# A third Strassen level for one of seven small products, with its sums on GpSimd

## Chip, cores and metric

The kernel runs on one core of a Trainium2 chip. The metric is device time in microseconds. Three runs of the kernel before took 819.62, 819.81 and 820.03 us; their median is 819.81 us.

## The reference

Everything is float32. For four sequences of 1024 tokens with 1024 features the kernel computes a layer norm, then two branches, a gated linear recurrence `s` and a two-expert routed feed-forward `ffn`, and returns `x + s * silu(ffn)`.

```python
xn = layernorm(x)
# recurrence branch
g   = sigmoid(xn @ gate_w.T + gate_b)
u_g = xn * g
aa  = tanh(a);  G = cumprod(aa over time)
s   = c * (G * cumsum(b * u_g / G_safe, time)) + (d + mean_t(u_g) @ d_lr_u @ d_lr_v / R) * u_g
# feed-forward branch
gates, idx = top2(softmax(xn @ wr.T)), normalised
h = silu(xn @ w1.T);  h = silu(h @ w3.T);  h = h @ w2.T
out = zeros;  for k in 0, 1:  out = out.at[idx[:, k]].add(gates[:, k] * h)
return x + s * silu(ffn)
```

The expert index addresses rows of the output, so only rows 0 to 7 of `out` receive anything. All other rows of the result are `x`. Those eight rows depend on all 4096 tokens through w1 and w3, and on the gate product of the first 1024.

## The kernel before

The tokens are taken in four groups of 1024 (`sb` 0 to 3, `NS = 4`). In each group there are two large products of 1024 x 1024 x 1024: `u` (times w1) and `m` (times w3). Group 0 also has `g` (times the gate weights). Each large product is done by Strassen's method in Winograd's form, twice nested.

**The outer level** makes seven products of 512 x 512 x 512 of each large one. The code calls each of them a Half. It has a kind, a group and an index i from 1 to 7, taken in the order `(1, 2, 5, 6, 7, 4, 3)` for u and `(1, 5, 6, 2, 7, 4, 3)` for m. Their left operands are blocks of tokens or the sums of blocks `s1` to `s4`; the right operands are blocks of weights or sums kept from group 0. A block is 128 partitions x 4 quarters x 512 elements.

**The inner level** makes seven small products of 256 x 256 x 256 of each Half, in the steps n = 0 to 6 of `Half.step`. Each is four matmuls of 128 x 128 x 256, issued by `small`. Left inner sums (`left_sums`, four per Half, on GpSimd) and right inner sums (computed in group 0, stored, and read back as quarters by `load_kept_sum`) are tiles of one quarter.

The small products go to PSUM banks. X takes steps 0, 2, 4 and 6 of a Half, Z steps 1 and 5, Y step 3. X and Z have two banks each, Y one. After each step VectorE (or, where a destination is new, ScalarE) reads the bank and adds it to the destination block (`first`, `more`). `whole` then runs the outer sums of the results, and SiLU on ScalarE when a quarter of the result is complete.

**The order** is written out by hand. Every engine's instructions keep the order in which the program emits them. A Half starts 7 places after the one before it, and its step n stands at its start + 2n, so two Halves interleave: the order of small products round a junction is step 6 of Half h-1 (place start + 5 of Half h), step 3 of Half h (start + 6), step 0 of Half h+1 (start + 7), step 4 of Half h (start + 8), step 1 of Half h+1 (start + 9). One place is one small product. The X bank of step 0 of Half h+1 is the one that step 6 of Half h-1 has used, and can be written once that step's result has been read. Work of the other engines is put between by `at(place, f)`: `left_sums` at start - 6, -4, 0 and +2, the loads of kept sums 9 places ahead of their use, and the outer sums of tokens `s1` to `s4` at places tied to the Halves that need them.

`s_engine` (line 779) says which engine makes the outer sums of the left side: GpSimd for u in groups 1 to 3, VectorE for the rest. In m of groups 1 to 3 these are 16 sums of 128 x 512 per group on VectorE.

Tiles of a block or a quarter come from two lists in rotation (`NB, NQ = 20, 18`, line 125). A released tile goes to the end of the list, and whoever takes it next waits for its last reader. All loads and stores of weights and tokens are issued on SP's queue, in order.

Of the kernel before, what the change touches and what calls it, by code (L numbers as in the profile page):

```python
# [10 lines left out]
F32 = mybir.dt.float32  # L11
# [3 lines left out]
ALU = mybir.AluOpType  # L15
AX = mybir.AxisListType
P = 128
Q = 256
# [4 lines left out]
def kernel(  # L23
# [55 lines left out]
    class Pinned:  # L79
# [15 lines left out]
    nc = tc.nc  # L95
    pe, dve, act, pool, sync = (
        Pinned(e) for e in (nc.tensor, nc.vector, nc.scalar, nc.gpsimd, nc.sync)
    )
# [7 lines left out]
    ps_y = ctx.enter_context(tc.tile_pool(name="ps_y", bufs=1, space=bass.MemoryType.PSUM))  # L106
# [15 lines left out]
            if self.uses == 0:  # L122
                self.home.append(self.tile)

    NB, NQ = 20, 18
    IDLE = 13
    blocks = deque(
        const.tile([P, 4, 2 * Q], F32, tag=f"b{i}", name=f"b{i}") for i in range(NB)
# [8 lines left out]
    def quarter(uses=1):  # L137
        return Held(quarters, uses)
# [47 lines left out]
    def at(place, f, *args):  # L186

        seq[0] += 1
        heapq.heappush(todo, (place, seq[0], f, args))
# [8 lines left out]
    def resume(p, g):  # L198
        step = next(g, None)
        if step is not None:  # L200
            at(p + step, resume, p + step, g)
# [14 lines left out]
    start = {}  # L216
# [301 lines left out]
    kept = {}  # L518
    op_t = {}
# [14 lines left out]
    def keep_quarter(name, i, j, o):  # L534
        d = dramp.tile([P, 2 * Q], F32, tag=f"{name}_{i}_{j}", name=f"{name}_{i}_{j}")
        sync.dma_start(d, o.tile)
        kept[name, i, j] = d
        o.drop()
# [177 lines left out]
    def first_w3():  # L716
# [48 lines left out]
    S_OF = {  # L765
        1: (0, 0),
        2: (0, 1),
        4: (1, 1),
        5: "s1",
        6: "s2",  # L770
        3: "s4",
        7: "s3",
    }
    left = {}
# [2 lines left out]
    A_AT = (1, 2, 4, 5)  # L777

    def s_engine(kind, sb):
        return pool if kind == "u" and sb > 0 else dve  # L780


    BANKS = {("u", 0): (0, 1), ("m", 0): (0,)}
# [1 line left out]
    def s1(kind, sb, n):  # L785
        eng = s_engine(kind, sb)
        a21, a22 = left[kind, sb, (1, 0)], left[kind, sb, (1, 1)]
        o = block(1 + n)
        if (kind, sb) in BANKS:
            yield from with_bank(o, a21, a22, (3, 0, 1, 2), op=ALU.add, of=BANKS[kind, sb])  # L790
        else:
            for q in (3, 0, 1, 2):
                eng.tensor_tensor(o[:, q], a21[:, q], a22[:, q], ALU.add)
                if q == 0:
                    yield 0.5
        a21.drop()
        a22.drop()
        left[kind, sb, "s1"] = o

    def s2(kind, sb, n):  # L800
        eng = s_engine(kind, sb)
        while (kind, sb, "s1") not in left:
            yield 0.25
        p, a11 = left[kind, sb, "s1"], left[kind, sb, (0, 0)]
        o = block(2 * n)
        if (kind, sb) in BANKS:
            yield from with_bank(o, p, a11, (2, 3, 0, 1), of=BANKS[kind, sb])
        else:
            for q in (2, 3, 0, 1):
                eng.tensor_tensor(o[:, q], p[:, q], a11[:, q], ALU.subtract)  # L810
                if q == 3:
                    yield 0.5
        p.drop()
        a11.drop()
        left[kind, sb, "s2"] = o

    def s4(kind, sb, n):

        eng = s_engine(kind, sb)
        while (kind, sb, "s2") not in left:  # L820
            yield 0.25
        o, a12 = left[kind, sb, "s2"], left[kind, sb, (0, 1)]
        if (kind, sb) == ("m", 0):
            yield from with_bank(o, o, a12, (2, 3, 0, 1), True, of=(0, 2))
        else:
            for q in (2, 3, 0, 1):
                eng.tensor_tensor(o[:, q], a12[:, q], o[:, q], ALU.subtract)
                yield 0.5
        a12.drop()
        left[kind, sb, "s4"] = o  # L830
# [35 lines left out]
                yield 2 * (A_AT[j + 1] - A_AT[j])  # L866


    def small(ps, A, B, start, stop, rows_first):

        for mt in range(2):
            for kt in range(2):
                w, m = (A, B) if rows_first else (B, A)
                pe.matmul(
                    ps[:, mt * Q : (mt + 1) * Q],
                    w[:, kt * Q + mt * P : kt * Q + (mt + 1) * P],
                    m[:, kt * Q : (kt + 1) * Q],
                    start=(start and mt == 0 and kt == 0),
                    stop=(stop and mt == 1 and kt == 1),
                    skip_group_check=True,  # L880
                )
# [3 lines left out]
    class Half:  # L885
# [30 lines left out]
        def whole(self, q):  # L916
            whole(self.kind, self.sb, self.i, q)

        def step(self, n):
            if n == 0:  # L920
                self.begin()
            A, t = self.A, self.t
            ts = [op_ts.get((self.kind, self.sb, self.i, j)) for j in range(4)]
            s = [left_q.get((self.src, self.sb, self.i, j)) for j in range(4)]

            def go(ps, a, b, start, stop):
                small(ps, a, b, start, stop, self.rows_first)

            if self.plain:

                q = ((0, 1, 2, 3) if self.i == 1 else (0, 3, 1, 2))[n // 2]
                ps = self.X if n // 2 % 2 == 0 else self.Z
                go(ps, A[:, q // 2 * 2 + n % 2], t[:, n % 2 * 2 + q % 2], n % 2 == 0, n % 2 == 1)
                if n % 2:
                    self.first(q, ps)
            elif n == 0:
                go(self.X, A[:, 0], t[:, 0], True, False)
                self.first(0, self.X)
            elif n == 1:
                go(self.Z, s[0].tile, ts[0].tile, True, False)  # L940
                self.first(3, self.Z)
                s[0].drop()
                ts[0].drop()
            elif n == 2:
                go(self.X, s[1].tile, ts[1].tile, False, False)
                self.first(1, self.X)
                s[1].drop()
                ts[1].drop()
            elif n == 3:
                Y = ps_y.tile([P, 2 * Q], F32, tag="Y", name=f"Y_{self.tag}")  # L950
                go(Y, A[:, 1], t[:, 2], True, True)
                if (self.kind, self.i) == ("g", 1):
                    at(Y_AT, self.more, 0, Y)
                else:
                    self.more(0, Y)
            elif n == 4:
                go(self.X, s[2].tile, ts[2].tile, False, False)
                self.more(3, self.X)
                s[2].drop()
                ts[2].drop()  # L960
            elif n == 5:
                go(self.Z, s[3].tile, t[:, 3], False, True)
                self.more(1, self.Z)
                s[3].drop()
            elif n == 6:
                go(self.X, A[:, 3], ts[3].tile, False, True)
                self.first(2, self.X)
                self.whole(2)
                ts[3].drop()
            if n == (7 if self.plain else 6):  # L970
                self.A.drop()
                t.drop()
# [265 lines left out]
    for kind, sb, i, plain in line:  # L1238
        h = Half(kind, sb, i, plain)
        halves.append(h)  # L1240
        S = start[kind, sb, i]
        n = 2 if sb == 0 and kind == "u" and i not in PLAIN_G else 1
        if kind != "g" and not plain:
            at(S + 2 - 8, left_sums, kind, sb, i, n)
        if kind != "g" and sb > 0:
            at(S - 10, load_kept, kind, sb, i)
            for j in range(4):
                at(S + 2 * T_AT[j] - 9, load_kept_sum, kind, sb, i, j)

    for sb in range(NS):  # L1250
        n = 2 if sb == 0 else 1
# [252 lines left out]
```

## Time and profile before

| | us |
|---|---|
| median of three runs | 819.81 |
| span of the profiled execution | 817.9 |
| start of u and of m in group 1 | 266.4 and 358.4 |
| start of u and of m in group 2 | 443.2 and 535.2 |
| start of u and of m in group 3 | 620.0 and 712.1 |
| one Half of u or m | 12.1 |

For the profiled execution the span alone is given; what lies around it is the difference to the times of the runs, 1.9 us.

The six stages of groups 1 to 3, from the profile's windows (columns: stretch, its length, busy microseconds and instructions of TensorE, weight loads, VectorE, ScalarE and GpSimd, granted TensorE clock, share of the DMA engines, GB/s):

```
266.00:358.00 92.00, 92.00 (x492) 78.00 (x490) 45.34 (x90) 39.76 (x74) 53.43 (x43) 1.00 0.67 243
358.00:443.00 85.00, 85.00 (x396) 74.67 (x395) 64.31 (x82) 17.01 (x29) 44.01 (x33) 1.00 0.76 285
443.00:535.00 92.00, 92.00 (x491) 78.04 (x490) 41.01 (x87) 39.27 (x72) 51.11 (x41) 1.00 0.62 228
535.00:620.00 85.00, 85.00 (x396) 74.64 (x396) 64.12 (x82) 16.82 (x29) 44.18 (x33) 1.00 0.77 286
620.00:712.00 92.00, 92.00 (x491) 78.03 (x490) 41.43 (x88) 17.92 (x30) 50.88 (x41) 1.00 0.56 194
712.00:797.00 85.00, 85.00 (x416) 73.02 (x415) 52.73 (x85) 14.24 (x24) 34.48 (x27) 1.00 0.46 167
```

A row of a group of instructions reads: line, engine, operation, what is written from what (buffer numbers left out), partitions x elements, count; then busy time and the mean duration of one in ns; then the engine's idle time just before them and what ended it. All lines of code show as line 89, that of the helper which records every operation, so tiles tell groups apart: q is a quarter, b a block, X, Y and Z with `_u`, `_m`, `_g` the banks of a kind. A matmul in float32 shows as two records on TensorE (PE) with two weight loads (PEld). A record lasts until its results have landed, so the next one starts before it ends.

### The profile page before, as it was taken

How to read it: one execution, taken by the hardware profiler on the slowest of the kernel's cores; microseconds unless marked ns; L12 is line 12 of the kernel's file. 1: busy time of each engine (PE TensorE's matmuls, PEld its weight loads, DVE VectorE, ACT ScalarE, POOL GpSimd, SP SyncE). 2: the span in 40 equal slices, each digit the busy share in tenths (PEclk: the TensorE clock that was granted, in tenths of full speed). 3: DMA queues.
4: the chain of work that ended last, by engine and by line, in shares of the span. 5: the costliest groups of instructions: out<-in, count | busy, mean ns of one | idle time of the engine just before them, and what ended most of it. 6: DMA issues, size and time to landing. Idle time of an engine off the chain costs nothing.

```text
span 817.9 us, 11299 instructions
## 1 busy us (share of the span) xinstructions
PE 810.6 (99%) x4085; PEld 696.5 (85%) x4085; DVE 509.7 (62%) x868; ACT 263.8 (32%) x458; POOL 496.1 (61%) x398
## 2 busy tenths in 40 slices
PE   8999999999999999999999999999999999999997
PEld 7888888888888878888888788888888788888885
DVE  6886598765588524764985235666983246667643
ACT  1245126877232237341022065421122021220111
POOL 2799896967999394744547453755448454465300
PEclk9999999999999999999999999999999999999999
DMA  9946619465978947629955875559666365555700
GB/s 338 421 175 232 230 47 357 171 246 160 411 267 309 345 174 293 241 103 385 376 179 210 332 279 190 187 206 426 242 244 257 104 219 203 196 180 195 283 14 2
DMA packets 55927, 192.88 MB, mean 236 GB/s; under 512 B 6480, under 2 KB 9792, under 8 KB 44224
## 3 DMA queue, kind: packets, MB, share of 16 engines
q1 hardware_dynamic: 55552, 191.61, 63.5%
q8 instruction: 33, 0.54, 0.3%
q10 hardware_dynamic: 320, 0.54, 0.2%
q14 instruction: 22, 0.18, 0.1%
HBM read 169.01 MB, written 39.87 MB: 255 GB/s over the span
## 4 chain that ended last, share of the span: by engine, by line
PE 98%; DMA 1%; DVE 0%; ACT 0%; issue 0%; SPq 0%
PE X_u L89 24%; PE X_m L89 24%; PE Z_u L89 12%; PE Z_m L89 12%; PE X_g L89 6%; PE Y_m L89 6%; PE Y_u L89 6%; PE Z_g L89 3%; PE acc L89 2%; PE plT L89 2%; PE Y_g L89 1%; DMA b<-in_x 1%; PE pp L89 0%; DVE bn L89 0%; PE accB L89 0%; PE ta L89 0%
## 5 line engine op out<-in xcount | busy, mean ns | idle before, releaser
L89 POOL TENSOR_TENSOR q<-b 128x512 f32<-128x512 f32 x154 | 203.0, 1331 | 193.7 <-PE X_m L89 48.0
L89 ACT ACTIVATE b<-b 128x512 f32<-128x512 f32 (+1 forms) x152 | 105.3, 696 | 298.1 <-DVE b L89 291.6
L89 POOL TENSOR_TENSOR q<-b,q 128x512 f32<-128x512 f32 x98 | 133.1, 1361 | 7.2 <-issue 4.0
L89 POOL TENSOR_TENSOR b<-b,b 128x512 f32<-128x512 f32 x72 | 92.9, 1310 | 48.5 <-PE X_u L89 33.7
L89 DVE TENSOR_TENSOR b<-b,b 128x512 f32<-128x512 f32 x120 | 109.2, 925 | 2.7
L89 PE MATMUL X_m<-q,q 128*128 128x256 f32 x448 | 105.9, 379 | 0.0
L89 PE MATMUL X_u<-q,q 128*128 128x256 f32 x432 | 102.4, 380 | 0.0
L89 DVE TENSOR_TENSOR b<-X_u,b 128x512 f32<-128x512 f32 x87 | 60.0, 690 | 57.8 <-PE X_u L89 57.1
L89 DVE TENSOR_TENSOR b<-X_m,b 128x512 f32<-128x512 f32 x88 | 60.4, 688 | 56.9 <-PE X_m L89 56.7
L89 PEld LDWEIGHTS X_m<-q,q 128*128 128x128 f32 x448 | 85.0, 190 | 12.4 <-issue 0.8
L89 POOL TENSOR_TENSOR q<-q,b 128x512 f32<-128x512 f32 x56 | 73.6, 1314 | 32.4 <-PE X_u L89 25.1
L89 PEld LDWEIGHTS X_u<-q,q 128*128 128x128 f32 x432 | 81.8, 190 | 12.2 <-issue 1.2
L89 DVE TENSOR_TENSOR b<-b,bc 128x1024 f32<-128x1024 f32 x56 | 67.8, 1211 | 0.1
L89 PE MATMUL X_u<-b,b 128*128 128x256 f32 x248 | 58.4, 380 | 0.0
L89 PE MATMUL Y_m<-b,b 128*128 128x256 f32 x224 | 53.1, 380 | 0.0
L89 PE MATMUL Z_m<-b,q 128*128 128x256 f32 x224 | 53.0, 380 | 0.0
L89 PE MATMUL X_m<-b,b 128*128 128x256 f32 x224 | 53.0, 379 | 0.0
L89 PE MATMUL Z_m<-q,q 128*128 128x256 f32 x224 | 52.9, 379 | 0.0
L89 PE MATMUL X_m<-q,b 128*128 128x256 f32 x224 | 52.9, 379 | 0.0
L89 PEld LDWEIGHTS X_u<-b,b 128*128 128x128 f32 x248 | 47.0, 190 | 6.7 <-DVE b L89 0.4
L89 DVE TENSOR_TENSOR b<-Z_u,b 128x512 f32<-128x512 f32 x47 | 32.4, 690 | 31.6 <-PE Z_u L89 30.7
L89 PE MATMUL Z_u<-q,q 128*128 128x256 f32 x216 | 51.1, 380 | 0.0
(182 smaller groups left out, 1171.6 us busy)
## 6 DMA issues: line engine op xcount, KB each, us to landing
q<-w SPq DMA_DIRECT2D x168, 256.0 KB, 4.5
b<-in_w SPq DMA_DIRECT2D x36, 1024.0 KB, 9.0
b<-w_T SPq DMA_DIRECT2D x24, 1024.0 KB, 6.3
b<-in_xT SPq DMA_DIRECT2D x15, 1024.0 KB, 12.9
w<-q SPq DMA_DIRECT2D x56, 256.0 KB, 7.4
b<-in_x SPq DMA_DIRECT2D x12, 1024.0 KB, 11.0
w_T<-b SPq DMA_DIRECT2D x8, 1024.0 KB, 4.4
b<-in_gw SPq DMA_DIRECT2D x6, 1024.0 KB, 14.0
```

What stands on the lines that cost most here:

```text
L89: r = f(*args, **kwargs)
```

## The change

In groups 1 to 3, for u and m, step 3 (the product `A[:, 1]` times `t[:, 2]`) is split once more by the same method: seven products of 128 x 128 x 128 in place of four matmuls of 128 x 128 x 256.

- `token_thirds` makes the left sums of the third level, three instructions on GpSimd (one of 128 x 256, two of 128 x 128), at start - 2. `weight_thirds` makes the right sums, four of 128 x 128 on GpSimd at start - 3, in group 1 alone, and stores them. `load_thirds` reads them back in groups 2 and 3 on SP's queue.
- `Half.eighth` issues the products: two at start + 2, ahead of step 1; one at start + 4, ahead of step 2; and four in place of step 3 at start + 6. All go to the Y bank, which the Half now holds from start + 2. VectorE adds parts of the bank to the destination: two reads of 128 x 128 after the first visit, one after the second, one of 128 x 512 and one of 128 x 128 after the third, in place of the one of 128 x 512.
- `s_engine` puts the outer sums of m in groups 1 to 3 on GpSimd too.
- There are 24 quarters in rotation for 18, and the scratch area for dynamic DMA is set to 1024 bytes.

Over the whole program that is 126 matmuls more, 168 VectorE reads of the bank more and 48 outer sums fewer, and 230 GpSimd sums more (48 outer ones, 182 of the third level); 42 transfers of 256 KB are added.

```diff
-    NB, NQ = 20, 18
+    NB, NQ = 20, 24
...
     def s_engine(kind, sb):
-        return pool if kind == "u" and sb > 0 else dve
+        return pool if sb > 0 else dve
...
+    def is_third(kind, sb, i):
+        return sb > 0 and kind != "g"
+
+    def cut(t):
+        return t.rearrange("p (k n) -> p k n", n=P)
+
+    def token_thirds(kind, sb, i):
+
+        a = cut(left[kind, sb, S_OF[i]][:, 1])
+        t = quarter()
+        o = cut(t.tile)
+        third_s[kind, sb, i] = t
+        pool.tensor_tensor(
+            o[:, 0:2], a[:, 1:2].to_broadcast([P, 2, P]), a[:, 0::3], ALU.subtract
+        )
+        yield 1
+        pool.tensor_tensor(o[:, 2], a[:, 0], o[:, 1], ALU.subtract)
+        pool.tensor_tensor(o[:, 3], a[:, 2], o[:, 2], ALU.subtract)
+
+    def weight_thirds(kind, sb, i):
+
+        name = {"u": "w1", "m": "w3"}[kind]
+        b = cut(op_t[kind, sb, i][:, 2])
+        t = quarter(2)
+        o = cut(t.tile)
+        third_t[kind, sb, i] = t
+        pool.tensor_tensor(o[:, 1], b[:, 1], b[:, 0], ALU.subtract)
+        yield 1
+        pool.tensor_tensor(o[:, 2], b[:, 3], o[:, 1], ALU.add)
+        pool.tensor_tensor(o[:, 3], b[:, 2], o[:, 2], ALU.subtract)
+        yield 1
+        pool.tensor_tensor(o[:, 0], b[:, 1], b[:, 3], ALU.add)
+        yield 1
+        keep_quarter(name, i, "t", t)
+
+    def load_thirds(kind, sb, i):
+        o = quarter()
+        sync.dma_start(o.tile, kept[{"u": "w1", "m": "w3"}[kind], i, "t"])
+        third_t[kind, sb, i] = o
...
+        def eighth(self, n):
+            key = self.kind, self.sb, self.i
+            a, b = cut(self.A[:, 1]), cut(self.t[:, 2])
+            S, T = cut(third_s[key].tile), cut(third_t[key].tile)
+            d = cut(self.dst[:, 0])
+            z, w = (1, 2) if self.rows_first else (2, 1)
+            if n == 0:
+                self.Y = ps_y.tile([P, 2 * Q], F32, tag="Y", name=f"Y_{self.tag}")
+            ps = cut(self.Y)
+
+            def go(o, p, q, start, stop):
+                left_side, right_side = (p, q) if self.rows_first else (q, p)
+                pe.matmul(
+                    ps[:, o], left_side, right_side, start=start, stop=stop, skip_group_check=True
+                )
+
+            def add(o, p):
+                dve.tensor_add(o, p, o)
+
+            if n == 0:
+                go(3, a[:, 0], b[:, 0], True, False)
+                go(z, S[:, 1], T[:, 1], False, False)
+                add(d[:, 0], ps[:, 3])
+                add(d[:, 3], ps[:, z])
+            elif n == 1:
+                go(3, S[:, 2], T[:, 2], False, False)
+                add(d[:, z], ps[:, 3])
+            else:
+                go(z, S[:, 3], b[:, 3], False, False)
+                go(w, a[:, 3], T[:, 3], False, False)
+                go(0, a[:, 2], b[:, 2], False, False)
+                go(3, S[:, 0], T[:, 0], False, True)
+                add(self.dst[:, 0], self.Y)
+                add(d[:, w], ps[:, 3])
+                third_s[key].drop()
+                third_t[key].drop()
+                self.whole(0)
...
+            elif n == 3 and is_third(self.kind, self.sb, self.i):
+                self.eighth(2)
...
+        if is_third(kind, sb, i):
+            for n, step in enumerate((2, 4)):
+                at(S + step, h.eighth, n)
+            at(S - 2, token_thirds, kind, sb, i)
+            at(S - 3, *((weight_thirds if sb == 1 else load_thirds), kind, sb, i))
...
-    nc = bacc.Bacc("TRN2", target_bir_lowering=False, num_devices=1)
+    nc = bacc.Bacc("TRN2", target_bir_lowering=False, num_devices=1, dynamic_dma_scratch_size=1024)
```

More of the change, by code (lines that the diff above doesn't have):

```diff
@@ L866, in left_sums @@
                 yield 2 * (A_AT[j + 1] - A_AT[j])
+    third_s = {}
+    third_t = {}
+    def is_third(kind, sb, i):
[31 more added lines that the diff above has]
+        third_t[kind, sb, i] = o
     def small(ps, A, B, start, stop, rows_first):
```

## The prediction

> **What bounds the kernel now.** I read the page's busy times and its chain of work that ended last, then who waited for whom on TensorE, then the timeline round a junction of two halves.
>
> ```profile
> PE 810.6 (99%) x4085; PEld 696.5 (85%) x4085; DVE 509.7 (62%) x868; ACT 263.8 (32%) x458; POOL 496.1 (61%) x398
> ...
> PE 98%; DMA 1%; DVE 0%; ACT 0%; issue 0%; SPq 0%
> ```
>
> ```profile
> PE idle L89 <- POOL eps L89: 1.6, 1, 1.6
> PE mean L89 <- DVE mv L89: 0.7, 1, 0.7
> PE scale L89 <- DVE rs L89: 0.3, 1, 0.3
> PE pp L89 <- DVE accT L89: 0.3, 1, 0.3
> ```
>
> TensorE is the bound everywhere: it waits 2.9 us in all, at the two ends. So each microsecond of matmul removed is a microsecond won, unless the shorter matmuls uncover a wait that was just covered. That second clause decides here.
>
> The price of the new matmuls is in the warm-up, which already runs f32 products of 128 columns:
>
> ```profile
> 8.64 0.75 PEld L89 LDWEIGHTS idle<-ident,ones 128*128 128x128 f32 x6
> 8.75 0.83 PE L89 MATMUL idle<-ident,ones 128*128 128x128 f32 x6
> ```
>
> An f32 matmul is two records. The six last 0.276 us each by the tile's own view (median 276 ns) and 0.83 together, so they start (0.83 - 0.276)/5 = 0.111 us apart, weight loads included. The products of 256 columns, and the junction where one half ends and the next but one begins, look like this:
>
> ```profile
> 427.63 1.89 PE L89 MATMUL X_m<-q,b 128*128 128x256 f32 x8
> ...
> 429.36 1.89 PE L89 MATMUL Y_m<-b,b 128*128 128x256 f32 x8
> 429.56 0.69 DVE L89 TENSOR_TENSOR b<-X_m,b 128x512 f32<-128x512 f32 x1 [0.27 <-PE X_m L89]
> ...
> 430.87 1.27 PEld L89 LDWEIGHTS X_m<-b,b 128*128 128x128 f32 x6
> ...
> 431.08 1.24 PE L89 MATMUL X_m<-b,b 128*128 128x256 f32 x5
> ```
>
> Eight records take 429.36 - 427.63 = 1.73 us. The X bank of the first row is read by VectorE from 429.56 to 430.25 and then rewritten by the X product of the last row, whose first weight load starts at 430.87: 0.62 us of slack. It exists because the Y product in between takes 1.73 us. The load does obey that wait. Round 394 us ScalarE (copying a bank) came late, and the load started 0.05 us behind its end:
>
> ```profile
> 394.09 0.58 ACT L89 COPY b<-X_m 128x512 f32<-128x512 f32 x1
> ...
> 394.72 1.38 PEld L89 LDWEIGHTS X_m<-b,b 128*128 128x128 f32 x7 [0.16 <-ACT b L89]
> ```
>
> **The change, part by part.** *TensorE.* In 42 halves (u and m, seven each, groups 1 to 3) the Y product of 8 records becomes seven products of 128 columns, 14 records: 14 x 0.111 = 1.55 us for 1.73. Removed: 42 x 0.17 (with the unrounded steps) = 7.2 us.
>
> *The new wait.* Of the 14 records two products stand ahead of step 1, one ahead of step 2, and only four products, 8 x 0.111 = 0.89 us, where the whole Y product stood. So in the junction above the X product is due at 429.36 + 0.89 = 430.25 and its weight load 0.11 earlier, at 430.14. VectorE's read still ends at 430.25, and the load may go 0.05 later, at 430.30: late by 0.16. With only 0.11 us between records the load has no slack, so TensorE loses all of it, and nothing else stands ahead of it in the queue. Of the 41 such junctions some 27 are freed by VectorE with this row's slack (0.62): 27 x 0.16 = 4.3 us. Nine are freed by a ScalarE copy of 0.58 (0.11 shorter): 9 x 0.06 = 0.5. The others have route or closing matmuls in between. Together 4.8 us. Four junctions have less slack now (0.05 near 394 and 571, 0.42 near 406 and 583), because ScalarE and VectorE were busy. If nothing improves there they lose 2 x 0.7 + 2 x 0.3 = 2.0. Part of what kept VectorE busy, the outer sums of m, leaves it, so I take 0.6 more, a little under half of what lies between. Sum of waits 5.4, ends 4.8 and 6.8.
>
> *VectorE.* Per half four added reads of 128 columns. None is shown; the nearest rows are 0.18 us (32 columns of a bank) and 0.42 (256). I take 0.25: 42 x 4 x 0.25 = 42 us, against 48 outer sums of m leaving at a mean of 0.9 (43 us). VectorE stays near 62%. Between the first and second visit to the Y bank, and between the second and third, two whole products (3.5 us) run, which cover 0.2 us for the product to land and two reads. Cost on the path 0; up to 1 us if reads take 0.42.
>
> *GpSimd.* The outer sums of m (16 per group) and the third-level sums: per half one of 256 and two of 128 columns, in group 1 also four of 128 for the weights.
>
> ```profile
> 358.00:443.00 85.00, 44.01 (x33) 1.00 0.76 285
> ...
> 535.00:620.00 85.00, 44.18 (x33) 1.00 0.77 286
> ```
>
> ```profile
> L89 POOL TENSOR_TENSOR q<-b 128x512 f32<-128x512 f32 x154 | 203.0, 1331 | 193.7 <-PE X_m L89 48.0 <-DVE b L89 37.4 <-PE Z_m L89 35.8
> ...
> L89 POOL MEMSET C<- 128x256 f32 x4 | 1.3, 316 | 0.0
> ...
> L89 POOL MEMSET ones<- 128x128 f32 x1 | 0.2, 204 | 0.0
> ```
>
> A sum of 128 columns is not shown. It lies between the memset (0.20) and the sum of 512 (1.33). A line through the one-column memset (0.098) and the 512-column sum where VectorE is not on SBUF (1.27) gives 0.39, and 0.69 for 256 columns. Per half of group 1: 0.69 + 6 x 0.39 = 3.0 us. The m stage of group 1 (windows above: GpSimd 44 of 85 us, some of it work ahead for the next group) then holds 28 inner sums, 16 outer sums and 7 x 3.0: 44 x 1.27 + 21 = 77 us of about 84. Groups 2 and 3 load the weight sums and have 66. The tight spot is the second half of m. From the first outer sum to what its first small products need, GpSimd has 12 sums of 512 (two back to back take 2.5 us) and five small ones: 15 + 2.3 = 17.3 us. They are due 9 products, 15.5 us, after m begins, so the outer sums must start 1.8 us before m does. Their first inputs are ready some 6 products earlier. I take 0, with some 3 us in hand. If that cover goes, TensorE waits for whatever GpSimd is late.
>
> [...]
>
> *DMA.* 42 more transfers of 256 KB: 14 stores in group 1, 28 loads later. SP issues each load 5 products before its first use; the quarters loaded now have 9. The stage of m in group 2 is the test: DMA share 0.77, and about 1.0 from 545 to 580 us while the next group's tokens come in. At 0.65 us per 256 KB of that full queue, two added loads push the load for the third half of m to within a microsecond of its use. Between 0 and 1.8 us; I take 0.2. Six more quarter buffers only turn the rotation, and the smaller scratch holds nothing here (no transfer starts on GpSimd's queue): 0, since nothing waits for either; with buffers the cover is the 24 in rotation against about 12 in use.
>
> **Sum.** -7.2 + 5.4 + 0.2 = -1.6 (by the ends of the waits -2.2 to -0.2). The span of 817.9 becomes 816.3. The runs' median of 819.81 lies 1.9 above the span, so the time is 818.2.
>
> **Rivals.**
> - *GpSimd becomes the bound in group 1 (slower).* For: 77 of 84 us and small sums nobody has timed. Against: its idle time of 282 us (193.7 + 7.2 + 48.5 + 32.4 in its four groups of sums) falls mostly in waits for buffers that TensorE still reads, and sums alongside VectorE's PSUM reads stay at 1.27. It decides once a small sum costs 0.39 + (84 - 77)/49 = 0.53 us. At 0.65 the m stage needs 90 us: 6 us late, 824.
> - *The added loads come late in m of group 2.* For: the full DMA queue. Against: the least lead of today's quarter loads there is 7 us. 2 to 4 us for the whole: about 821.
> - *The wait is not paid.* If VectorE's read is released earlier than 0.89 us after the product, most of 7.2 stays: about 814. For: only 0.16 us separates the two. Against: 0.2 for the landing and 0.69 for the read are fixed in every row looked at.
> - *The 128-column products do not run at 0.111.* Weight-load records last 0.19 us. At 1.73/14 = 0.123 nothing is won, and the waits remain: about 825. Against: the warm-up did it at full clock with loads in between.
>
> **Numbers.** A change within 0.2% (1.6 us) can't be told from none here. The forecast (gain mostly given back at the junctions) has 0.60 and its own range is 816.8 to 820.0, which straddles the limit of 818.2: 0.33 faster, 0.27 same. Wait not paid 0.09, faster. GpSimd 0.15 (0.13 slower, 0.02 same). Late loads 0.12 (0.07 slower, 0.05 same). Slow small products 0.04, slower. That makes 0.42, 0.34, 0.24. The range runs from 815.5 (part of the wait unpaid) to 823.5 (most of GpSimd's case).
>
> **What would show it.** Y_m and Y_u as 14 records 0.11 us apart; a weight load of X behind VectorE's b<-X by about 0.16 us of TensorE idleness at most junctions, 5 to 6 us in all among TensorE's waits; GpSimd near 9 tenths busy in m of group 1 without TensorE waiting for it; VectorE without b<-b,b sums in m. It is wrong if TensorE's waits name GpSimd or DMA, if the junction wait is absent or far over 0.16, or if small GpSimd sums last over 0.5 us.

## The result, and the profile after

| kernel | median, us | executions | ratio to the kernel before |
|---|---|---|---|
| before | 819.6 | 818.9 to 820.6 | |
| changed | 821.4 | 819.4 to 822.4 | 1.0018 [1.0009, 1.0026] |
| changed, a second set | 822.3 | 821.0 to 822.8 | 1.0033 [1.0020, 1.0046] |

The forecast was 818.2; the changed kernel is 0.2 to 0.3% slower than the one before, not faster. The profiled execution took 821.7 us, its span is 819.9 (817.9 before).

The page of the changed kernel, busy times and the head of the chain that ended last:

```profile
PE 811.4 (99%) x4337; PEld 701.8 (86%) x4337; DVE 519.2 (63%) x988; ACT 263.9 (32%) x458; POOL 642.1 (78%) x628
...
PE 93%; DMA 4%; DVE 2%; SPq 0%; issue 0%; ACT 0%
```

TensorE has 252 records more (126 matmuls of two) and is busy 0.8 us longer, though the new products are shorter work. GpSimd has gone from 61 to 78%. Who waited for whom on TensorE:

```profile
PE idle L89 <- POOL eps L89: 1.6, 1, 1.6
PE Y_m L89 <- DVE b L89: 0.3, 1, 0.3
PE pp L89 <- DVE accT L89: 0.3, 1, 0.3
PE Y_m L89 <- DMA q<-w_t: 0.2, 1, 0.2
PE X_u L89 <- DMA b<-in_w: 0.2, 1, 0.2
PE acc L89 <- DVE rs L89: 0.2, 1, 0.2
```

Two new waits at Y products of m, small; the waits at an X product of u and at `acc` stand in the first 18 us, ahead of the changed part. At the X products of groups 1 to 3 there is nothing. The wait that the forecast is about is not in this list. It hides in the rows of a junction (columns: start, length, engine, operation, tiles, shapes, count, and in brackets the idle time before):

```profile
429.02 1.89 PE L89 MATMUL X_m<-q,b 128*128 128x256 f32 x8
...
430.21 1.44 DVE L89 TENSOR_TENSOR b<-X_m,b 128x512 f32<-128x512 f32 x2
...
430.75 0.39 PE L89 MATMUL Y_m<-b,q 128*128 128x128 f32 x2
...
431.42 0.39 PE L89 MATMUL Y_m<-q,q 128*128 128x128 f32 x2
...
431.70 1.59 PEld L89 LDWEIGHTS X_m<-b,b 128*128 128x128 f32 x8
431.70 1.99 PE L89 MATMUL X_m<-b,b 128*128 128x256 f32 x8
```

VectorE's second read of an X bank in the row of two ends at 430.21 + 1.44 = 431.65, and the weight load to that bank starts 0.05 us behind it. In the row of the kernel before (430.87 and 431.08) the first load starts 0.21 us ahead of its product; here load and product start together, and the eight records take 1.99 us where they took 1.89. TensorE is never idle by the records (one of 256 columns lasts 0.38 us and the next starts 0.216 behind it, so they overlap), so no list of waits shows the loss. It shows in the groups, as a longer mean record of X products of blocks, the step-0 products:

```profile
L89 PE MATMUL X_u<-b,b 128*128 128x256 f32 x248 | 60.1, 386 | 0.3 <-DMA b<-in_w 0.2
L89 PE MATMUL X_m<-b,b 128*128 128x256 f32 x224 | 54.6, 386 | 0.0
```

Before, these groups took 58.4 us (mean 380 ns) and 53.0 (379); all other X groups are as they were. To add it up, the start of each matmul was set against the start of the one before it plus that one's undisturbed step (0.432 us for 256 columns, 0.223 for 128, two records each). Time beyond the step, from 266 us on:

| where TensorE lost time | before | changed |
|---|---|---|
| junctions: first X product behind a Y product | 0 | 5.3 |
| Y visits, all but the next row | 0.2 | 2.0 |
| Y visits, waiting for a load of third-level weight sums | 0 | 0.4 |
| elsewhere | 1.7 | 1.7 |
| sum | 1.9 | 9.4 |

In the second row the 0.2 of before stands at the second record of two Y products in group 3, and is there in both kernels; the 1.8 that came are waits for VectorE's read of the Y bank. The loss that the change adds, 7.5, outweighs the shorter matmuls' 6.9. With 0.2 more ahead of 266 us the last matmul starts 0.8 us later. The remaining 1.2 us of the 2.0 that the span grew lie behind the last matmul.

Behind the growth of the second row stands VectorE's queue. The second visit of Half 2 of m in group 1 starts with the weight load at 402.24:

```profile
399.23 1.37 DVE L89 TENSOR_TENSOR b<-b,b 128x512 f32<-128x512 f32 x1
400.52 1.21 DVE L89 TENSOR_TENSOR b<-b,bc 128x1024 f32<-128x1024 f32 x1
401.65 0.47 DVE L89 TENSOR_TENSOR b<-Y_m,b 128x128 f32<-128x128 f32 x2
```

```profile
398.28 0.30 PEld L89 LDWEIGHTS Y_m<-q,q 128*128 128x128 f32 x2
...
402.24 0.30 PEld L89 LDWEIGHTS Y_m<-q,q 128*128 128x128 f32 x2 [0.41 <-issue]
```

The first visit's products ended near 398.8. VectorE reads them three microseconds later, from 401.65 to 402.12, since a sum of two blocks and a product of the next group's norm stand ahead in its queue, and the load follows 0.12 behind. That is 0.2 us of loss at the first record and 0.07 more at the second; it is the commonest kind at the Y visits. (Losses of single visits are given below for the first record, sums with both.)

GpSimd in m of group 1 (columns as in the table of stages above), and the new small operations:

```profile
358.00:443.00 85.00, 84.85 (x433) 74.34 (x432) 60.12 (x94) 16.84 (x28) 83.83 (x96) 1.00 0.83 306
```

```profile
L89 POOL TENSOR_TENSOR q<-b,q 128x128 f32<-128x128 f32 x112 | 55.7, 500 | 5.8
L89 POOL TENSOR_TENSOR q<-b 128x256 f32<-128x256 f32 x42 | 30.7, 730 | 14.9 <-PE X_u L89 14.9
L89 POOL TENSOR_TENSOR q<-b 128x128 f32<-128x128 f32 x28 | 13.3, 474 | 0.0
...
L89 DVE TENSOR_TENSOR b<-Y_m,b 128x128 f32<-128x128 f32 x84 | 22.1, 283 | 0.7
```

GpSimd is busy 83.8 of 85 us, full; yet each of its sums is ready before the matmul that needs it, with 1.05 us in hand at the tightest place and over 3 at all others. A sum of 128 columns takes 0.47 to 0.50 us, and one that needs the sum just before it starts 0.08 later.

### The profile page after: what moved, and what is told of

Same layout as the page of the kernel before. It is cut to its first block, busy times and chain, and to the rows that moved or that the text cites. A ratio compares the mean times of both kernels' runs of the same rounds, so it can differ in the third digit from the quotient of the medians.

```text
span 819.9 us, 12318 instructions
## 1 busy us (share of the span) xinstructions
PE 811.4 (99%) x4337; PEld 701.8 (86%) x4337; DVE 519.2 (63%) x988; ACT 263.9 (32%) x458; POOL 642.1 (78%) x628
## 4 chain that ended last, share of the span: by engine, by line
PE 93%; DMA 4%; DVE 2%; SPq 0%; issue 0%; ACT 0%
PE X_u L89 23%; PE X_m L89 22%; PE Z_u L89 12%; PE Z_m L89 11%; PE X_g L89 6%; PE Y_u L89 5%; PE Y_m L89 5%; PE Z_g L89 3%; PE acc L89 2%; PE plT L89 2%; DMA q<-w_t 1%; PE Y_g L89 1%; DMA b<-in_x 1%; DMA q<-w 1%; DVE b L89 1%; DVE s L89 0%
## 5 line engine op out<-in xcount | busy, mean ns | idle before, releaser
L89 POOL TENSOR_TENSOR q<-b 128x512 f32<-128x512 f32 (+2 forms) x224 | 243.6, 1105 | 63.8 <-DVE b L89 22.9
L89 POOL TENSOR_TENSOR b<-b,b 128x512 f32<-128x512 f32 x120 | 152.9, 1292 | 64.2 <-PE X_u L89 29.0
L89 POOL TENSOR_TENSOR q<-b,q 128x128 f32<-128x128 f32 (+1 forms) x210 | 185.8, 889 | 8.2 <-PE X_u L89 2.2
L89 PEld LDWEIGHTS X_m<-q,q 128*128 128x128 f32 x448 | 83.3, 190 | 11.3 <-issue 0.8
L89 DVE TENSOR_TENSOR b<-X_m,b 128x512 f32<-128x512 f32 x88 | 60.1, 687 | 50.7 <-PE X_m L89 50.0
L89 DVE TENSOR_TENSOR b<-b,b 128x512 f32<-128x512 f32 x72 | 72.6, 1011 | 3.0
L89 PE MATMUL X_u<-b,b 128*128 128x256 f32 x248 | 60.1, 386 | 0.3 <-DMA b<-in_w 0.2
L89 DVE TENSOR_TENSOR b<-Y_m,b 128x128 f32<-128x128 f32 (+1 forms) x112 | 41.3, 384 | 21.0 <-PE Y_m L89 20.2
L89 DVE TENSOR_TENSOR b<-Y_u,b 128x128 f32<-128x128 f32 (+1 forms) x111 | 40.6, 381 | 18.0 <-PE Y_u L89 17.3
L89 PEld LDWEIGHTS X_u<-b,b 128*128 128x128 f32 x248 | 45.3, 190 | 7.4 <-DVE b L89 1.0
```

What stands on the lines that cost most here:

```text
L89: r = f(*args, **kwargs)
```

## The experiments

Theory 1 was that the gain is real and goes back mainly at the junctions. The rivals were GpSimd's added load, VectorE's added reads, and the added transfers.

**The junction wait taken away.** Step 0 of Half h+1 comes behind step 4 of Half h, so that 0.89 + 1.73 us stand between the product and the next one to its bank.

```diff
-        (... else start[kind, sb, i] + 2 * n, k, n)
+        (... else start[kind, sb, i] + 2 * n + (1.5 if sb > 0 and n == 0 else 0), k, n)
```

> The changed kernel with one order changed in groups 1 to 3: step 0 of Half h+1 comes behind step 4 of Half h instead of ahead of it, so the X bank's read by VectorE is covered by the four small Y products and a whole X product (0.89 + 1.73 us) instead of 0.89 alone. Theory 1 (the late weight load at the junctions costs about 5.3 us): TensorE's loss at Y to X and inside the first X product falls from 5.7 us to under 1, the time from 821.4 to about 816, below the 819.6 of the kernel before. If GpSimd's outer sums of m or the added transfers are what eats the gain: unchanged, 821 to 822. If the extra VectorE reads are: unchanged too, with the loss at the Y visits.

817.34 us, ratio to the kernel before 0.9973 [0.9965, 0.9982]; 4 us less than the changed kernel, and faster than both. The groups of step-0 products in this kernel:

```profile
L89 PE MATMUL X_u<-b,b 128*128 128x256 f32 x248 | 58.4, 380 | 0.0
...
L89 PE MATMUL X_m<-b,b 128*128 128x256 f32 x224 | 52.9, 379 | 0.0
```

The stretch is gone, and the junctions lose 0.1 us together. The time is over a microsecond short of 816, because the Y visits now lose 4.1 in place of 2.4 us. The largest, 1.4 us, is the second visit of Half 6 of m in group 3:

```profile
736.82 3.53 DVE L89 TENSOR_TENSOR_SCAN s<-aab,bu 128x8 f32<-128x8 f32 x4
...
741.80 0.49 DVE L89 TENSOR_TENSOR b<-Y_m,b 128x128 f32<-128x128 f32 x2
```

```profile
740.40 1.02 POOL L89 TENSOR_TENSOR q<-b,q 128x128 f32<-128x128 f32 x2
...
742.40 0.30 PEld L89 LDWEIGHTS Y_m<-q,q 128*128 128x128 f32 x2 [1.62 <-POOL q L89]
```

The bracket names GpSimd, and misleads. The load waits for two things by the program: VectorE's reads of the first visit, which end at 741.80 + 0.49 = 742.29, 0.11 ahead of it, and a small sum of GpSimd's that was done at 729.3. The GpSimd row above, which ended last ahead of the load, is for another Half. VectorE is late because the recurrence's scans run here, 0.88 us each for the 0.23 of the profile before, beside GpSimd's sums. TensorE is earlier, so more of VectorE's queue comes to light. Several of the expectations below call these waits GpSimd's, as the bracket does; that reading fell.

**The same order without a third level.**

> The kernel before with step 0 of Half h+1 behind step 4 of Half h in groups 1 to 3, without a third level. Here the whole Y product covers the X bank's read already (0.62 us in hand). Theory 1: the other order is worth nothing by itself, 819.0 to 820.2, so its 4 us in the changed kernel are the junction wait. If the order helps in another way: 815 to 817.

819.88, ratio 1.0003 [0.9995, 1.0012]. The order alone is worth nothing; in the changed kernel it takes away the 5 us at the junctions, of which the later Y visits give back 1.7. (By the two profiles 0.9 us of the difference lies behind the last matmul.)

**The short gap without a third level.** The Y product of groups 1 to 3 keeps two of its four matmuls (the first half of its contraction); the rest is the kernel before.

```diff
-                go(Y, A[:, 1], t[:, 2], True, True)
...
+                    for mt in range(2):
+                        pe.matmul(
+                            Y[:, mt * Q : (mt + 1) * Q],
+                            w[:, mt * P : (mt + 1) * P],
+                            m[:, 0:Q],
...
```

> The kernel before with the Y product of groups 1 to 3 cut to its first contraction half: two of its four matmuls are left out, and nothing else is changed. This removes 42 x 0.863 = 36.2 us of matmul and leaves 0.86 us between the step-6 product and the next product to the same X bank, as the changed kernel does with its four small ones, but with no third level, no added sum, read or transfer. Theory 1: the junction wait appears here too, 0.16 to 0.19 us at 27 to 30 junctions and less at 9 others, 5 to 6.5 us given back: 788.5 to 790 instead of 783.4. If the wait comes from what the third level adds to the other engines: 783 to 785.

792.31: 27.3 us gained of 36.2, so 8.9 came back, more than the 5 to 6.5 expected. One of its junctions:

```profile
410.28 1.28 DVE L89 TENSOR_TENSOR b<-X_m,b 128x512 f32<-128x512 f32 x2
...
410.54 1.03 PE L89 MATMUL Y_m<-b,b 128*128 128x256 f32 x4
...
411.61 1.59 PEld L89 LDWEIGHTS X_m<-b,b 128*128 128x128 f32 x8 [0.45 <-DVE b L89]
411.61 1.99 PE L89 MATMUL X_m<-b,b 128*128 128x256 f32 x8
```

The same picture: the load 0.05 us behind VectorE (410.28 + 1.28 = 411.56), 1.99 for 1.89. The wait needs no third level, only the gap. The usual junction loses 0.19 us, as expected; that the sum is 9 and not 6.5 comes from ten junctions, nine of them in m, at which VectorE or ScalarE is late (0.26 to 0.42, and two of 0.88). VectorE still makes the outer sums of m here.

**The move of the outer sums alone**, in the kernel before, and **the move undone**, in the changed kernel (the same line back):

```diff
-        return pool if kind == "u" and sb > 0 else dve
+        return pool if sb > 0 else dve
```

> The kernel before with the one part of the change that moves the outer sums of m to GpSimd, without a third level. Theory 1: the move alone costs nothing, 819.3 to 820.1, as without the third level's sums GpSimd has 7 x 3 us less in m of group 1. If GpSimd's slower sums hold TensorE up: 821 or more, with waits of TensorE on GpSimd at m's second Half.

> The changed kernel with the 48 outer sums of m back on VectorE. Theory 1: the junctions lose the same, about 5.3 us, or more where VectorE is late because of the sums (up to 1 us); the three waits on GpSimd ahead of Y visits (0.9 us together) go; 820.3 to 822. If GpSimd's load is what eats the gain: 816 to 818.

Alone it costs nothing: 819.71, ratio 1.0001 [0.9992, 1.0010]; GpSimd has 58.7 busy us of 85 in m of group 1. (In the profile before, a 128 x 512 sum of two blocks took 1.31 us on GpSimd and 0.93 on VectorE in the mean.) Undone it makes the changed kernel slower: 824.11, ratio 1.0051 [1.0038, 1.0063], outside what either theory gave. VectorE then has 68.7 busy us of 85 in that stage (60.1 in the changed kernel), the Y visits lose 4.8 us in all for 2.4, and the junctions 0.8 more, nearly all of it at one (1.1 us near 409). The third level's reads need the time that the outer sums of m leave on VectorE. The first run clears the move of the sums, not the fuller GpSimd of the changed kernel; that one is cleared by the first experiment, which leaves all its work on GpSimd and is 4 us faster, and by the sums' being ready in time. The rival of VectorE's reads is half right: with the outer sums moved they cost about 2 us, without that over 4.

**No third level where its visits are late.** With the new order, first without Half 6 of u and m, then also without Half 2 of m in group 1:

```diff
-        return sb > 0 and kind != "g"
+        return sb > 0 and kind != "g" and i != 6
...
+        return sb > 0 and kind != "g" and i != 6 and (kind, sb, i) != ("m", 1, 2)
```

> The changed kernel with step 0 behind step 4 as in the first experiment, and without the third level in Half 6 of u and m in groups 1 to 3 (their Y product is the whole one again). It gives up 6 x 0.164 = 1.0 us of matmul. In the first experiment TensorE lost 0.9 us at the Y visits of Half 6 of u, 1.5 at that of m in group 3 and 0.6 at that of Half 2 of m in group 1, where GpSimd has been busy without a pause since m began. Theory 1, with the second half that these are waits for sums not ready: 817.3 + 1.0 - 0.9 - 1.5 - 0.6 = 815.3. If the waits only move to the next Half: 817.5 to 818.5.

> The second group's kernel without the third level in Half 6, and without it also in Half 2 of m in group 1, where TensorE still waited 0.85 us for GpSimd; that Half's third-level weight sums for groups 2 and 3 are made 5 places later. It gives up 0.16 us. Theory: 815.85 + 0.16 - 0.85 = 815.2. If GpSimd's lateness moves on to Half 7: 815.8 to 816.5.

815.85 (815.65 to 816.59), ratio 0.9959 [0.9946, 0.9972], the fastest complete kernel of the study beside the next one, and 0.5 us over the 815.3 expected. The time nearly fits, the reason given does not. At the late Y visits of these kernels the product follows VectorE's read of the Y bank by 0.13 to 0.16 us, and GpSimd's sum has long been done: at Half 2 of m in group 1, where 0.85 us were still lost (0.61 in the first experiment, and the expectation had none), the sum was ready at 392.5, the read at 401.7, the product at 401.9. Without that Half's third level this wait went too, but 0.40 us appeared at Half 4, again behind VectorE's read, and the time stayed: 815.95, ratio 0.9959 [0.9946, 0.9971]. That misses the 815.2 expected and lies in the range of the other case, but what moved on is VectorE's lateness, and to Half 4. What remains in m of group 1 is VectorE's queue.

**The loads of third-level sums earlier**, and **the changed kernel again**:

```diff
-            at(S - 3, *((weight_thirds if sb == 1 else load_thirds), kind, sb, i))
+            at(*((S - 3, weight_thirds) if sb == 1 else (S - 7, load_thirds)), kind, sb, i)
```

> The changed kernel once more, to see which part of its 821.4 us is the same in every execution. Expected: 820.8 to 822; the junctions again 5.5 to 5.9 us and the Y visits 2 to 3; the 6.5 us from the last matmul to the end of the span, against 5.3 in the kernel before, may come out anywhere between 5.2 and 6.6 if it is the landing of the last transfers.

> The changed kernel with the loads of the third level's weight sums in groups 2 and 3 issued 7 places ahead of their Half and not 3; nothing else. In the two profiles of the changed kernel TensorE waited 0.4 and 1.0 us for the one of Half 6 of m in group 2. Theory: that wait goes, the junctions stay (5.7 us): 820.7 to 821.5. If the added transfers matter more than that one wait shows: below 820.5.

The second set of the changed kernel, 822.3, is a little over the 822 expected. Its profile has the junctions within 0.1 us of the first, but its wait for a load is 1.0 where the first had 0.4:

```profile
PE Y_m L89 <- DMA q<-w_t: 0.9, 1, 0.9
```

It is the load for Half 6 of m in group 2 in both. Issued 4 places earlier it is not waited for, and the kernel takes 820.63, just under the 820.7 to 821.5 of the theory and over the 820.5 of the other case. Its ratio, 1.0016 [1.0007, 1.0025], can't be told from the 1.0018 of the changed kernel's first set. From the start of u in group 1 to the last matmul its profile has 547.4 us, the two of the changed kernel 547.5 and 547.8: where the wait for the load went, waits for VectorE's reads came (0.3 us at a visit near 579 us, which had none). So the transfers cost at most what that one wait shows, and how much of it an earlier issue wins is not shown.

**The third level in u alone**, with the new order, and two runs on what it brought up.

```diff
-        return sb > 0 and kind != "g"
+        return sb > 0 and kind == "u"
```

> The changed kernel with step 0 behind step 4, and the third level in u alone; the outer sums of m stay on GpSimd. This gives up 21 x 0.164 = 3.4 us of matmul in m and saves the 3.2 us that TensorE lost at the Y visits of m in the first experiment. Theory: 817.3 + 3.4 - 3.2 = 817.5, so the third level in m earns nothing even with the junctions mended, because GpSimd is full there. If GpSimd's load costs nothing: 820.8.

Four executions took 817.6 to 818.0, as expected: with the junctions mended, m's third level earned nothing over u's alone, its shorter matmuls against VectorE's late reads (the Y visits lose 1.0 us in this profile for 4.1 in the first experiment). The other eight took 822 to 832, and the profile is of one of them (826.1). In its timeline, m of group 3:

```profile
724.72 16.56 DVE L89 TENSOR_TENSOR uv<-lrv_sb,rk 128x32 f32<-128x32 f32 x1
...
741.16 0.32 POOL L89 MEMSET b<- 128x256 f32 x1
741.32 0.19 DVE L89 TENSOR_REDUCE pd<-uv 128x8 f32<-128x32 f32 x1
...
743.92 2.21 PEld L89 LDWEIGHTS Z_m<-q,q 128*128 128x128 f32 x6 [6.50 <-issue]
743.95 2.47 PE L89 MATMUL Z_m<-q,q 128*128 128x256 f32 x5 [6.13 <-issue]
```

A VectorE product of 32 columns, 0.18 to 0.69 us in the profiles so far, takes 16.56 while GpSimd runs 13 sums of 512 columns without a pause, and ends as GpSimd comes to a memset. TensorE waits for VectorE's read of a Z bank, 6.1 us by this row and 6.3 by the starts of the matmuls. In the next run one operand of that product comes from PSUM:

```diff
-        dve.tensor_mul(uv, lrv_sb, rk.unsqueeze(1).to_broadcast([P, KD, R]))
+        dve.tensor_mul(uv, lrv_sb, pr.unsqueeze(1).to_broadcast([P, KD, R]))
```

> The third run's kernel (third level in u alone, step 0 behind step 4) with one operand changed: VectorE's product of lrv_sb and rk takes its second operand from the PSUM bank that rk is copied from, so that it has one SBUF input and not two. In the profile of the slow execution this 128x32 product took 16.56 us while GpSimd issued 13 sums without a gap, and TensorE then waited 6.3 us for VectorE. Theory (two SBUF inputs kept out while GpSimd runs): no execution over 818.6, median 817.6. If the stall comes from elsewhere: again 817.6 in some executions and 822 to 832 in others.

The expectation on the time failed: 816.8 to 817.7 in four executions, 825 to 829 in eight. The profile says why. With one operand from PSUM the product took 0.18 us, and the next instruction with two SBUF inputs took 16.10 instead:

```profile
724.44 0.18 DVE L89 TENSOR_TENSOR uv<-lrv_sb,pr 128x32 f32<-128x32 f32 x1
724.65 0.19 DVE L89 TENSOR_REDUCE pd<-uv 128x8 f32<-128x32 f32 x1
724.87 16.10 DVE L89 SCALAR_TENSOR_TENSOR deff<-pd,vec_sb 128x8 f32<-128x8 f32 x1
```

In the last run a memset of one column stands behind GpSimd's inner sums and those of `s1` and `s2` in m of group 3:

```diff
             left_q[kind, sb, i, j] = o
+            if (kind, sb) == ("m", NS - 1):
+                pool.memset(gap, 0.0)
...
                 eng.tensor_tensor(o[:, q], a21[:, q], a22[:, q], ALU.add)
+                if (kind, sb) == ("m", NS - 1):
+                    pool.memset(gap, 0.0)
...
```

> The kernel with the third level in u alone and step 0 behind step 4, where 12 of 17 slow executions so far... the profile showed one VectorE instruction with two SBUF inputs kept for 16 us while GpSimd ran sums without a gap, until GpSimd came to a memset. Here a memset of one column stands behind each inner sum and each sum of s1 and s2 of m in group 3 on GpSimd; nothing else is changed. Theory: VectorE gets its turn at the first memset, no execution over 818.6, median 817.6 to 818. If the pause of GpSimd isn't what frees VectorE: again some executions at 817.6 and others at 825 to 832.

(The count at the head of this expectation is a slip: 16 of the 24 executions of the two kernels were over 820 us.) Again the time missed: 817.1 to 826.6, median 822.3. The 16 us did go. The product now ends with the next memset, 0.1 us behind its start:

```profile
727.02 1.05 DVE L89 TENSOR_TENSOR uv<-lrv_sb,rk 128x32 f32<-128x32 f32 x1
727.97 0.10 POOL L89 MEMSET gap<- 128x1 f32 x1
728.02 1.27 POOL L89 TENSOR_TENSOR q<-q,b 128x512 f32<-128x512 f32 x1
...
729.24 1.38 DVE L89 TENSOR_SCALAR first<-aa 128x8 f32<-128x8 f32 x1
...
735.51 1.36 DVE L89 COPY aab<-aa 128x64 f32<-128x64 f32 x1
```

But of the small VectorE instructions behind it thirteen wait too, each until a sum of GpSimd's ends: nine end with a memset, three between two sums without one, one behind the last of the sums. TensorE still waits 3.2 us for VectorE there, and 2.2 us in m of group 1, where no memset was added and one VectorE instruction took 5.0. Why some executions have the stall and others not stays open.

## Why the prediction was wrong

- **TensorE, -7.2.** Right: 126 matmuls added and the products at the warm-up's step. The records start 0.1116 us apart for the rounded 0.111, and 42 x 0.164 = 6.9.
- **The new wait, +5.4.** Right in place, and in size for the usual junction: 27 junctions lose 0.16 to 0.18 us or, three of them, 0.23 to 0.24; nine lose 0.05; the others next to nothing. Sum 5.2 to 5.3. Of the four irregular ones near 394, 571, 406 and 583 us, those of ScalarE lose 0.05 each, the others 0.24 and 0.16: most of VectorE's and ScalarE's lateness went with the outer sums of m. So of the 0.6 taken for them on top of the usual loss only 0.1 came, and that the sum fits is partly luck: two other junctions, near 310 and 609 us, lose 0.23 and 0.24, and the usual ones a little over 0.16. What the forecast said of its showing was wrong: it does not come as idleness in the list of waits but as longer records.
- **VectorE, 0. This is the step that failed.** The reads take 0.283 for the 0.25 taken, and VectorE is 63% busy as forecast. But "two whole products (3.5 us) run, which cover 0.2 us for the product to land and two reads" left out what VectorE has queued ahead of the reads: a sum of blocks (up to 1.8 us beside GpSimd), a norm product (1.21), two reads of other banks (0.69 each). And the Y bank passes from one Half to the next with a read in between, which the forecast didn't look at: 0.16 us at Half 6 of u in each group. Together 1.8 us (1.5 in the second profile) where the forecast had nothing, and 3.9 once the junctions are mended.
- **GpSimd, 0.** The path cost was right, the working was not. The line between a memset and a 512-column sum gave 0.39 and 0.69 where 0.50 and 0.73 were measured, and nothing for the 0.08 between dependent sums, so "77 of 84" was 83.8 of 85 and "some 3 us in hand" was 1.05 at the least. The rival's threshold of 0.53 per small sum was nearly reached, but the rival did not come in. GpSimd's part is indirect: the scans of the recurrence on VectorE take 0.74 us each beside its sums in m of group 3, where they took 0.23 before; in the second profile they take 0.38, and the largest wait at a Y visit of the first, 0.4 us near 745, is not there.

```profile
L89 DVE TENSOR_TENSOR_SCAN s<-aab,bu 128x8 f32<-128x8 f32 x8 | 5.6, 744 | 0.0
```

- **DMA, 0.2.** The right load, the right stage, too small: the wait is 0.4 and 1.0 us in the two profiles.
- **Nothing else, 0.** Behind the last matmul the changed kernel needs 1.2 us more. In the last 3.9 us of its span the view of the DMA queues has a packet of the kind "instruction", which before has none there:

```profile
q14 instruction: 1, 0.01, 0.9%
```

  The last output transfer is issued 2.15 us ahead of the end of the span before, 3.34 and 3.19 in the two profiles after. Five profiles of kernels built on the changed one have such a packet, with 2.48 to 3.34 us; those without it have 2.34 to 2.44, and the four built on the one before 2.14 to 2.16. That this packet causes the delay was not tried; the cause stays open. What the smaller scratch area does no run tried either: that it holds nothing was the author's inference from the list of DMA issues, all of them on SP's and ScalarE's queues before and after.

Sum, with 0.2 ahead of 266 us: -6.9 + 5.3 + 1.8 + 0.4 + 0.2 + 1.2 = 2.0, the growth of the span; the forecast had -1.6. Of the 3.6 between them, half is VectorE's late reads and one third the end of the program. The profiled execution then took 1.8 us more than its span, as taken. The two large terms, of opposite sign, were each within 0.3 us, so their difference could only be as good as the small ones.

## What to carry to other kernels

When a product is shortened, list what its length covered: here a bank's read by VectorE, and moving one small product across a junction won back 4 us that no list of waits showed. The reads added to VectorE, 63% busy here, waited behind what stood ahead of them in its queue (3 us at Half 2 of m in group 1), so count the queue between the product and the next write to its bank, not the share. And when a bracket names an engine, look up what the waiting instruction needs: the one named here had been done for 13 us.

## What the runs showed of the hardware

**A late weight load cost time at two places.** In the usual junction (the one at 431.70 us above) the first record started 0.06 us late and the second record 0.10 later still, 0.16 in all; from the third on the records stood 0.216 us apart again. More than half of the loss showed one record behind the late load.

**VectorE instructions lasted through many of GpSimd's sums in a row.** The 16.56 and 16.10 us above are the extreme. VectorE's sums of two blocks took 0.67 to 1.80 us in the profile before and 0.68 to 1.76 in the one after, and one in the run with the memsets took 5.0. With one operand in a PSUM bank nothing of the kind shows: all 88 of its reads of the X banks of m took 0.67 to 0.69 us in the same two profiles, and the product above took 0.18. But two SBUF inputs are not what all the long ones have in common: a scalar operation and a copy with one took 1.38 and 1.36 in the run with the memsets, where they took 0.16 and 0.19 behind the stall in the first of the three runs. Nor does one sum of GpSimd's, 1.27 us, set the length: 13 ran in a row beside the 16.56 us, and in the run with the memsets most of the long instructions ended at a memset or between two sums. What keeps VectorE waiting was not shown.

**A stall cost more than its length.** After those 6 us without matmuls the granted clock was half for 4 us (stretch, length, busy times, then clock, DMA share and GB/s):

```profile
738.00:743.90 5.90, 0.00 (x0) 0.00 (x0) 5.76 (x8) 0.00 (x0) 4.70 (x5) 0.79 0.03 6
743.90:747.90 4.00, 3.95 (x9) 3.19 (x10) 3.02 (x15) 0.00 (x0) 0.00 (x0) 0.50 0.84 283
```

Matmuls of 256 columns started 0.85 us apart there for 0.43, which added 2.2 us to the 6.3 of the wait. In the run with the memsets the clock was 0.50 for 3 us as well, 1.2 us after the end of the stall of 3.2; behind the stall of 2.2 it stayed at 1.00.
